# Weighted diagonals of a top-4 expert layer: made by GpSimd between its row gathers instead of by ScalarE

## The chip, the cores and the metric

The kernel runs on one core of a Trainium2 chip. The metric is the device time of one execution in microseconds (us); the kernel before took 1272.82 us, the median of three runs (1269.32 to 1274.13).

The engines are named as the profile names them: PE is TensorE, DVE is VectorE, ACT is ScalarE, POOL is GpSimd and SP is SyncE, which only starts transfers here. Each engine works through one queue in order. An instruction that waits holds up everything behind it on its own engine and nothing on the others, except those that need its result.

## The reference

The input is 2 sequences of 2048 rows of 128 numbers (float32). Three steps follow one another, each with a residual connection:

```
x = x + 0.5 * ffn(layernorm(x))      # first expert layer
x = x + ssm(layernorm(x))            # state space layer, 2 x 128 channels, 16 states
x = x + 0.5 * ffn(layernorm(x))      # second expert layer, same weights

# ffn, per row: 32 experts, 4 chosen
scores = softmax(row @ router_w.T + router_bias)
top4, idx = top_k(scores, 4);  top4 = top4 / top4.sum()
out = sum_k top4[k] * down[idx[k]](silu(gate[idx[k]] row) * up[idx[k]] row)
out = out + shared_expert(row)

# ssm: a scan along the sequence, per channel d and state s
h[d,s] = h[d,s] * exp(dt[d] * A[d,s]) + dt[d] * u[d] * B[s]
y[d]   = sum_s h[d,s] * C[s] + D[d] * u[d]
```

The scan carries its state from row to row, so the two sequences are each worked through in order. The expert layers have no such chain, but the experts of a group of rows can run only when all of its rows are sorted, and the results of a group can be collected only when all of its experts are done.

## The kernel before

The 4096 rows are 8 blocks of 512 (blocks 0 to 3 are the first sequence, 4 to 7 the second). A block is 4 tiles of 128 rows.

**An expert layer** (`mixture`, from line 689) handles the blocks in groups: (0,1), (2,3), (4,5,6,7) in the first layer and (0,1,2,3), (4,5), (6,7) in the second. For each group:

- PE makes the router's scores and DVE picks the best four and works out, for every row and choice, a slot in a list sorted by expert (lines 735 to 927). The weights `wk` of the four choices come out of this too.
- POOL writes every row to its four slots in memory: one indirect transfer per tile and choice, 128 rows each (`scatter`, L948; 16 per block, 256 in all).
- The experts run over the sorted list, four slots of 128 rows at a time: SP loads the rows (L1038) and the weights of the slots' experts (`fetch`, L1057, two experts into one buffer `wt`, of which there are 8), PE turns and multiplies (L1075, L1085, L1113), ACT and DVE apply silu and the product (L1097, L1103), SP stores the result (L1126).
- POOL fetches for every tile its four result rows, one indirect transfer per choice (`gather`, L1140; 256 in all), into `yg`.
- The four results of a row are weighted and added on PE: `weighed` (L1165) multiplies each gathered 128x128 block by a diagonal matrix that has the weights of that choice on its diagonal, and lets PSUM add the four products. The diagonal is the identity with each partition scaled by its weight. Four of them make a buffer `dg`, of which there are 2. `diagonal` (L1157) makes them on ACT, four activations per tile, 256 in all.
- DVE adds the sum to the block (L1176) and, in the first layer, takes the statistics for the next layernorm.

**The state space layer** (`state_space`, from line 1215) goes block by block. ACT and POOL make the steps `dt` and `dtu` (on POOL the three operations L1357 to L1359, twice per block). Then 16 states follow. For each, SP brings a row of B to all partitions (L1379), POOL multiplies it with `dtu` into a buffer `hst` (`drive`, L1389; 128 in all; 4 buffers), ACT makes the decays (L1401), DVE runs two scans (L1427) and one product (L1440), and PE adds the result to the output (L1206), which frees the buffer.

**The order.** No engine's order comes from a scheduler at build time. Every step is an operation of a planner (`op`), and the list `ORDER` (lines 48 to 242) gives the sequence in which all of them are issued. `RINGS` (line 39) gives the number of buffers of each kind. The steps that matter here are spread through the whole list: gathers and scatters stand between drives, and the expert layers overlap the state space layer at both of its ends.

**Pads.** A planner operation with a lag (scatter and gather) counts up a row; any other POOL operation sets it back to 0. From the third transfer in a row on, a small memset of a scratch tile (`pad`, L414) is put ahead of the transfer:

```
            if o.eng == "pool":
                row = row + 1 if o.lag else 0
                o.pause = row > 2
```

Of the kernel before, what the change touches and what calls it, by code (L numbers as in the profile page):

```python
# [13 lines left out]
ALU = mybir.AluOpType  # L14
# [6 lines left out]
TOPK = 4  # L21
# [4 lines left out]
TB = 4  # L26
# [15 lines left out]
    shb=1, sg=3, hs=4, xs=4, xT=3, h=3, wt=8, yq=3, yg=4, dg=2,  # L42
# [6 lines left out]
0 36 1 104 10 27 31 16 6 8 13 5 20 7 22 9 4 12 49 14 2 30 11 25 120-121 3 80 17 37 26 97 32 19 92 28 23 79 48 15 24  # L49
18 21 107 29 100 50 38 89 40 39 33 83 122-123 129-132 124 81 34 58 41 91 43 96 42 35 98 885-886 884 133 887 45-46  # L50
59-60 85 87 47 88 44 51 84 52 114 78 56 54 82 86 53 55 90 110 95 57 112 93 125-128 134-136 138 137 888 186-189 139
190-195 198 196 199 197 200 140 201 889 142 141 143-144 202-203 145-146 890-892 204-205 208 206 895 207 210 900 209
211-213 216 214 217-218 147 150 215 896 901 219 151-153 220-221 897 902 893-894 503 61 101 94 996 998 898-899 905
997 1000-1001 999 1002 1004 1003 502 1006 1005 1008-1010 1007 1011 906 903 148 904 907-908 149 99 909-910 504-506
911 1012-1013 912 1014 1016 1015 1017 915 1018 1020 1019 1021-1022 1024 1023 1026-1027 1025 1028-1030 916 914 913
917 1031 154 168 184 164 167 177 163 176 165 174 170 159 181 172 169 155 157 162 156 158 175 178 173 179 185 180 171
160 183 166 182 161 223 237 222 224 236 251 250 238 918-919 1032 1034 1033 1035-1036 1038 1037 1039-1040 1042 1041
1044-1045 921 1043 1046 511 1047 920 1048 922-924 1049 225 512 925-926 928 927 513 226 507 239 230 508 240 231-232
253-254 241-242 244 227 245 243 246 252 258 255 228 256 229 233 259 234 257 260 929-931 247 264 267 265 278 71
292-293 266 66 279 248 261-262 268 281-282 295-296 269-270 283-285 271 294 249 306 514-515 272-273 297-298 274 299  # L60
280 235 286-288 263 72 75 320 568 509 275 450 570 276 510 516 569 571 289 300-302 290 517 303-304 518-519 572 574
573 309-310 576 575 578 577 580-581 579 520-521 582-583 307 311-313 321 70 68 335 74 69 291 106 308 277 64 305 77
334 62 67 336 63 348 322 102 76 349 65 73 363 362 323 584 522 324 585 524 523 525-526 325-327 314-315 527-528 316
328-330 337-338 342-343 351 317-318 352 344 339-340 365-366 341 331-332 116 376 350 379-380 345 356 346 319 390 377
364 113 347 333 111 378 404 418 353-354 357 367-368 529 532 358 393 369 355 359 394 360 370-372 381-383 586 588
373-374 587 590 589 592 384 591 593 385-386 530 594 596 595 531 597 387-388 407 598 600 408 432 103 419 391 395-396
405 117 420 392 361 397 421 599 601 422 398-400 533 435-436 409-410 401 423-424 402 433 406 105 389 434 375 411-413
426-427 414 425 428 415-416 932 995 982 946 958 976 988 947 942 933 989 939 935 959 953 937 936 963 950 993 954 957
943 974 956 949 944 941 990 960 969 977 965 951 948 962 536 945 952 955 564 543 555 546 552 558 566 550 565 557 562
540 559 538 561 539 560 553-554 541 563 545 544 537 549 547 551 548 556 567 542 429-430 440 437 109 605 403 619 417  # L70
620 431 108 602 457 438 441-442 439 443-445 460 961 463 455 470 447 461 469 448 456 446 449 462 453-454 468 467 968
973 940 603-604 618 606 633 632 1050 1052 1051 1053-1058 1060 1059 1062 1061 1063-1067 607 621 608 622 609-611
626-627 612-613 628 614 646 660 647 661 634-635 623-625 636 615 629 649 616 630 650 663-664 640 637 641-642 674 648
631 662 688 702 617 675 651 638-639 652-656 665-666 668-670 667 451 677 119 691 678 464 692 452 458 643-644 657 459
471 465-466 658 671 705 472-473 706 672 1516-1517 679 689-690 676 703 716 645 693 115 659 704 673 730 696 680 694
681-682 697 1518 534 698 695 683 719 1519 478 720 684 710-711 1520 712 685 1521 492 686 1522-1524 699 707-708 700
744 1529-1530 758 731-732 717 1531 718 709 1525 1532 1526 474 483 476 938 491 495 484 934 481 475 482 477 994
488-489 971 497 490 981 966 498 496 713 733-734 714 1536 1533-1535 1537 479 1527-1528 747 485 480 748 724-725 486
1538 487 726 1539 1542-1544 1540 715 118 687 772 745-746 701 786 1550 1560 759-760 735 738 721 739 736 722 535 1545
740 737 723 1541 1546-1547 987 1551 761-762 727-728 493 741 775 494 499 776 500 742 501 729 1570 800 773-774 980  # L80
1561 986 975 1571 992 814 1580 801 1581 1590 1552-1553 749-750 766-767 839 751-753 1554-1555 768 1556-1557 754
763-764 1562 755 1563 789 1564 765 769 1548 756 1558 1720 790 1565-1567 1574 1572 1721 770 1568 1573 1575-1577 780
1549 777 1559 1569 803 1722 1582-1583 781 984 972 1591 802 815 1600 757 1610 771 787 743 1620 964 1601 970 979 1630
788 778 1584-1586 779 1587 782 1578 1592 1594 791 1579 1593 1595-1597 804 1602-1603 1605-1606 1723 1604 1589 1599
1607 1588 792 1612 783-784 1608 1598 1613 1724 1611 967 983 793 817 1614-1617 1621 985 1631 991 978 1622 818 1623
794 805 808 795 809 806 1625-1626 796 810 807 1632 1609 1619 1624 1627 797 811 816 1725 1634 798 1633 1635-1637 812
1642 1628 1618 1643 1097 1640 1069 1641 1650 1660 785 1070 799 1670 1068 1082 822-823 1645-1646 1651 819 1629 820
1726 1638-1639 1644 824 821 1647 1652 825 1655 1071 1654 1649 1085 826 1653 1648 1656 1072 1662-1663 1661 1665-1666
1729 1657 1086 1672 1671 1673 1727 1076 1664 1730 1667 1659 1073 1077 1658 1728 1074 1674 1733 1675-1676 1078 1075
1677 1682 1680 813 1681 1685 827 1683 1734 1079-1080 1736 1690 1096 1700 1692 1740 1678 1741-1742 1110 1735 1111  # L90
1124 1138 1081 1083 1754 1684 1686-1687 1669 1679 1689 1737-1738 1668 831 836 838 835 828-830 1691 851 837 1694 1099
1695 1743 1739 1746 1693 1100 1744 832 1696-1697 833 1704 1702 1747-1748 1699 1113-1114 1688 1703 834 1701 1705 1749
840-841 844 1764 1084 1098 1774 1087 1706 1090 1707 1104 1750 1088 1091 846 1745 843 1751 845 1755 842 849-850 852
1765 1709 853 1710 1105 1715 1092 1089 1106 1101-1102 1711-1712 1103 1756 1708 1757 1716-1717 1758 1093 1713
1759-1761 1718 1714 1719 1698 1094 1752 1766 1731 1767 1762 1732 847-848 1769-1770 1768 1753 1115 854 1763 1127 860
1116 1784 856 866 1775 871 855 1117 1771 1776 1924 1777 867 1925-1926 1128 1778-1781 1786 1772 1107 1787 1927 1108
1928 1794 1804 1773 1783 1141 1152 1788 1785 880 1795 1805 865 1789-1791 1796 1142 1782 1797 1929-1932 1798-1801
1806 1937 1808 1807 1809-1811 1938 1940 1792 1816 1944 1793 1945 1802 1817 1814 1125-1126 1112 1824 1815 859 863
857-858 1825 879 864 1129 1132 1139 1939 1109 1834 1166 1844 1854 1818-1821 1941 1130 1133 1118-1120 1131 1134
1826-1827 1829-1830 1803 1155 1813 1169 861 1823 1828 1835 1822 1812 1942-1943 1836 1156 1839 1831 862 1946 1170  # L100
1837 868 872 1845 1855 877 1840 1846 1121 1950 881 874 1122 1847 869 1832 1951 1864 1095 1180 1153 1140 1154 1874
1884 1194 870 873 878 1833 1838 1849-1850 1841 1933 1856 1952 1857 1842 1934 1135 1848 1143-1144 1859 1851 1866 1858
1843 1860 1145 1861 1953 1867 1862 1136 1954 1865 1157 1868 1935 1869-1871 1947 1875-1876 1158 1852 1936 1877 875
1853 1159 1879 876 882-883 1880 1886 1955 1146-1147 1160 1863 1878 1161 1123 1894 1167-1168 1904 1181 1208 1885 1137
1222 1182 1895 1889 1148 1162 1881 1887 1890 1873 1149 1183 1888 1408 1896 1872 1150 1184 1891 1897 1163 1948 2128
1164 1882 1898 1197 1174 1883 1899-1901 1906-1907 1198 1188-1189 1175 1905 1949 1893 1908 1171 1903 1172 2129
# [216 lines left out]
def macaron_kernel(  # L323
# [23 lines left out]
    nc = tc.nc  # L347
# [335 lines left out]
    def mixture(li, gi):  # L683
# [449 lines left out]
        for i, b in enumerate(blocks):  # L1133
            for t in range(TB):
# [20 lines left out]
                def diagonal(i=i, t=t, dg=dg):  # L1155
                    for k in range(TOPK):
                        nc.scalar.mul(  # L1157
                            dg.t[:, k, :], ident.t, route["wk"][:, i * TB + t, k : k + 1]
                        )
# [429 lines left out]
```

## Time and profile before

| | us |
|---|---|
| median of three runs | 1272.82 |
| the profiled execution, its own time | 1270.85 |
| its span (first to last instruction) | 1269.1 |
| PE busy | 999.6 |
| POOL busy | 996.7 |
| DVE busy | 853.0 |
| ACT busy | 817.2 |

The span is 1.75 us shorter than the execution's own time. Three of the POOL groups, out of the list of groups: 128 drives take 303.4 us, 382 pads 125.6 us and 256 gathers 247.1 us. On ACT the 256 diagonals take 80.7 us.

How such lines are read: "busy" is the time in which an engine's instructions ran, without its waits and its register work. A group is all instructions of one line and shape, with its summed time, the mean of one in nanoseconds, and the idle time of the engine just before its instructions with the work that ended that idle time. The chain of waits follows the end of the program back, at each step to what released it. The timeline lists one engine's instructions with the idle time ahead of each in square brackets; "issue" there means that the engine waited for nothing that the profile shows.

### The profile page before, as it was taken

How to read it: one execution, taken by the hardware profiler on the slowest of the kernel's cores; microseconds unless marked ns; L12 is line 12 of the kernel's file. 1: busy time of each engine (PE TensorE's matmuls, PEld its weight loads, DVE VectorE, ACT ScalarE, POOL GpSimd, SP SyncE). 2: the span in 40 equal slices, each digit the busy share in tenths (PEclk: the TensorE clock that was granted, in tenths of full speed). 3: DMA queues.
4: the chain of work that ended last, by engine and by line, in shares of the span. 5: the costliest groups of instructions: out<-in, count | busy, mean ns of one | idle time of the engine just before them, and what ended most of it. 6: DMA issues, size and time to landing. Idle time of an engine off the chain costs nothing.

```text
span 1269.1 us, 20680 instructions
## 1 busy us (share of the span) xinstructions
PE 999.6 (79%) x6276; PEld 811.2 (64%) x6290; DVE 853.0 (67%) x1567; ACT 817.2 (64%) x1578; POOL 996.7 (79%) x1088
## 2 busy tenths in 40 slices
PE   5968797877788787877858767588788886978986
PEld 3637676766566676765535545365678875868864
DVE  6764432259889999996499999999998534312221
ACT  3514442798798887975857866668788554535542
POOL 0768788899898655668899999878688358888886
PEclk9988998989898898998979897789899989989997
DMA  9899996886636674851213323132689987799932
GB/s 328 274 307 329 328 295 193 263 247 202 199 107 192 179 227 137 276 156 47 72 33 99 107 73 104 61 100 80 189 253 303 287 246 230 239 311 287 301 106 70
DMA packets 255985, 248.61 MB, mean 196 GB/s; under 512 B 24961, under 2 KB 223234, under 8 KB 255874
## 3 DMA queue, kind: packets, MB, share of 16 engines
q1 hardware_dynamic: 239490, 213.70, 54.6%
q0 software_dynamic: 16384, 33.59, 8.7%
q8 instruction: 51, 0.84, 0.3%
q14 instruction: 60, 0.49, 0.1%
HBM read 177.72 MB, written 69.47 MB: 195 GB/s over the span
## 4 chain that ended last, share of the span: by engine, by line
DVE 30%; PE 20%; POOL 14%; DMA 13%; ACT 9%; issue 9%; SPq 4%; POOLq 0%; DVEq 0%; ACTq 0%
DVE hst L1427 15%; POOL yg L1140 7%; PE gu L1085 7%; DVE hst L1440 4%; POOL pad L414 3%; PE oq L1113 3%; DMA yg<-ys,idx 3%; POOL xs L948 3%; PE sum L1165 3%; DMA wt<-w_dram 3%; ACT L420 2%; ACT da L1401 2%; DMA xs<-xs 2%; PE pt_x L1075 2%; DVE h L1103 2%
## 5 line engine op out<-in xcount | busy, mean ns | idle before, releaser
L1389 POOL TENSOR_TENSOR hst<-dtu,bs 128x1024 f32<-128x1024 f32 x128 | 303.4, 2377 | 70.2 <-PE y L1206 22.9
L1140 POOL DMA_INDIRECT yg<-ys,idx x256 | 247.1, 965 | 78.1 <-issue 40.1
L1085 PE MATMUL gu<-xT,wt 128*128 128x128 f32 x1792 | 249.7, 293 | 24.3 <-DMA wt<-w_dram 10.3
L1085 PEld LDWEIGHTS gu<-xT,wt 128*128 128x128 f32 x1792 | 234.0, 207 | 45.8 <-DVE h L1103 12.4
L948 POOL DMA_INDIRECT xs<-xn,idx x192 | 192.6, 1003 | 81.4 <-DMA hst<-in_up_w 34.1
L1427 DVE TENSOR_TENSOR_SCAN hst<-da,st,hst 128x512 f32<-128x512 f32 x192 | 237.5, 1269 | 5.3 <-ACT da L1401 3.0
L1401 ACT ACTIVATE da<-dt,a 128x512 f32<-128x512 f32 x256 | 174.6, 690 | 58.3 <-DVE hst L1427 55.2
L1103 DVE TENSOR_TENSOR h<-sgq,gu 128x256 f32<-128x256 f32 x224 | 88.6, 417 | 174.3 <-ACT sgq L1097 172.1
L420 ACT ACT_TABLE_LOAD x134 | 171.9, 1283 | 3.2 <-PEq L1577 0.8
L1206 PEld LDWEIGHTS y<-ident,hst 128*128 128x128 f32 x1024 | 127.7, 151 | 70.1 <-issue 38.0
L1440 DVE TENSOR_TENSOR hst<-hst,c 128x1024 f32<-128x1024 f32 x128 | 156.0, 1219 | 12.7 <-PE c L1413 2.7
L1206 PE MATMUL y<-ident,hst 128*128 128x128 f32 x1024 | 142.4, 289 | 25.0 <-DVE hst L1440 23.1
L1097 ACT ACTIVATE sgq<-gu 128x256 f32<-128x256 f32 x224 | 81.0, 384 | 117.5 <-PE gu L1085 113.9
L1113 PE MATMUL oq<-wt,h 128*128 128x128 f32 x896 | 125.1, 286 | 20.4 <-DVE h L1103 16.7
L1113 PEld LDWEIGHTS oq<-wt,h 128*128 128x128 f32 x896 | 113.4, 198 | 32.5 <-DVE h L1103 21.6
L414 POOL MEMSET pad<- 128x256 bf16 x382 | 125.6, 329 | 0.3
L1165 PE MATMUL sum<-yg,dg 128*128 128x128 f32 x512 | 85.7, 320 | 44.5 <-DMA yg<-ys,idx 34.2
L1165 PEld LDWEIGHTS sum<-yg,dg 128*128 128x128 f32 x512 | 78.3, 228 | 54.9 <-DMA yg<-ys,idx 19.8
L1075 PE MATMUL pt_x<-ident,xs 128*128 128x128 f32 x448 | 73.1, 294 | 43.2 <-DMA xs<-xs 28.1
L1078 ACT COPY xT<-pt_x 128x512 f32<-128x512 f32 x112 | 65.0, 584 | 50.4 <-PE pt_x L1075 50.1
L1157 ACT ACTIVATE dg<-ident,wk 128x128 f32<-128x128 f32 x256 | 80.7, 391 | 22.6 <-PE sum L1165 20.1
L1075 PEld LDWEIGHTS pt_x<-ident,xs 128*128 128x128 f32 x448 | 56.5, 152 | 56.6 <-DVE h L1103 15.8
(148 smaller groups left out, 1504.4 us busy)
## 6 DMA issues: line engine op xcount, KB each, us to landing
wt<-w_dram SPq DMA_DIRECT2D x448, 192.0 KB
bs<-bd SPq DMA_DIRECT2D x128, 256.0 KB
xs<-xs SPq DMA_DIRECT2D x112, 256.0 KB
ys<-yq SPq DMA_DIRECT2D x112, 256.0 KB
xs<-zero SPq DMA_DIRECT2D x56, 256.0 KB
w_dram<-hst SPq DMA_DIRECT2D x12, 512.0 KB
yg<-ys,idx POOLq DMA_INDIRECT x256
xs<-xn,idx POOLq DMA_INDIRECT x192
```

What stands on the lines that cost most here:

```text
L414: pool(nc.gpsimd.memset(pad, 0.0))
L420: nc.scalar.preload_act_table_set(name)
L948: nc.gpsimd.indirect_dma_start(out=xs_b.t, out_offset=bass.IndirectOffsetOnAxis(ap=route["idx"][:, i * TB + t, k : k + 1], axis=0), in_=xn ...
L1085: nc.tensor.matmul(gu.t[:, j, s, :], wt.t[:, s, j * H : (j + 1) * H], xT.t[:, s0 + s, :], start=True, stop=True,)
L1113: nc.tensor.matmul(o.t[:, s, :], h.t[:, s, :], wts[s // 2].t[:, s % 2, 2 * H :], start=True, stop=True,)
L1140: nc.gpsimd.indirect_dma_start(out=yg.t[:, k, :], out_offset=None, in_=ys_b.t, in_offset=bass.IndirectOffsetOnAxis(ap=route["idx"][:, i * ...
L1165: nc.tensor.matmul(sm_.t, dg.t[:, k, :], yg.t[:, k, :], start=(k == 0), stop=(k == TOPK - 1),)
L1206: nc.tensor.matmul(y[:, t, k * P : (k + 1) * P], src[:, k, t * P : (t + 1) * P], ident.t, is_transpose=True, start=start and k == 0 and t ...
L1389: nc.gpsimd.tensor_tensor(h.t[:, :, 1:], dtu.t, bs.t.unsqueeze(1).to_broadcast([P, ND, T]), ALU.mult)
L1401: nc.scalar.activation(da.t, dt.t[:, k, :], AF.Exp, scale=a_t.t[:, k, s : s + 1])
L1427: nc.vector.tensor_tensor_scan(h.t[:, k, 1:], da.t, h.t[:, k, 1:], 0.0 if ini else st_sb[:, k, s : s + 1], ALU.mult, ALU.add,)
L1440: nc.vector.tensor_tensor(h.t[:, :, :T], h.t[:, :, 1:], cb.t.unsqueeze(1).to_broadcast([P, ND, T]), ALU.mult,)
```

## The change

`diagonal` is issued on POOL instead of ACT, as four planner operations per tile instead of one, so that each of the four can stand between two transfers. Since a diagonal has no lag, it sets the row of transfers back, and pads fall away where it stands. `dg` gets 4 buffers instead of 2, `wt` 7 instead of 8, and the whole list `ORDER` is another one (the indices in it are new, because there are 192 more operations).

```diff
-    shb=1, sg=3, hs=4, xs=4, xT=3, h=3, wt=8, yq=3, yg=4, dg=2,
+    shb=1, sg=3, hs=4, xs=4, xT=3, h=3, wt=7, yq=3, yg=4, dg=4,
...
-0 36 1 104 10 27 31 16 6 8 13 5 20 7 22 9 4 12 49 14 2 30 11 25 120-121 3 80 17 37 26 97 32 19 92 28 23 79 48 15 24
+0 13 1 10 104 12 4 7 27 8 11 5 25 6 2 37 86 9 29 19 17 82 22 100 21 15 23 101 28 16 24 18 36 14 20 26 105 3 88 48 97
...
-                def diagonal(i=i, t=t, dg=dg):
-                    for k in range(TOPK):
-                        nc.scalar.mul(
-                            dg.t[:, k, :], ident.t, route["wk"][:, i * TB + t, k : k + 1]
+                for k in range(TOPK):
+
+                    def diagonal(i=i, t=t, k=k, dg=dg):
+                        pool(
+                            nc.gpsimd.tensor_scalar(
+                                dg.t[:, k, :],
+                                ident.t,
+                                route["wk"][:, i * TB + t, k : k + 1],
+                                None,
+                                ALU.mult,
+                            )
                         )
 
-                op("act", 1.1, diagonal, r=[wk_b, route_b], w=[dg])
+                    op("pool", 0.5, diagonal, r=[wk_b, route_b], p=[dg])
```

What the built program holds on POOL: 256 diagonals more and 115 pads instead of 382; drives, scatters and gathers are the same in number. On ACT the 256 diagonals are gone and there are 138 loads of activation tables instead of 134.

Some counts that the list alone does not show, from the built queue of POOL. "Behind" is the number of transfers that stand directly behind another transfer.

| stretch of POOL's queue | before: transfers / behind / pads / diagonals | after |
|---|---|---|
| first scatter to first drive | 146 / 1 / 143 / 0 | 148 / 27 / 88 / 32 |
| first drive to drive 28 | 46 / 12 / 11 / 0 | 44 / 7 / 0 / 33 |
| drive 28 to the first gather of group (4,5,6,7) | 0 / 0 / 0 / 0 | 0 / 0 / 0 / 10 |
| that gather to drive 64 (block 4) | 51 / 3 / 45 / 0 | 47 / 7 / 3 / 37 |
| drive 64 to drive 112 | 77 / 25 / 6 / 0 | 81 / 14 / 5 / 19 |
| drive 112 to the first gather of the second layer | 32 / 6 / 19 / 0 | 32 / 7 / 11 / 9 |
| that gather to the last gather | 160 / 1 / 158 / 0 | 160 / 44 / 8 / 111 |

On DVE, PE and ACT the order hardly moves against the scans: the DVE work issued ahead of any of the landmarks (every eighth state) differs by 3.5 us at most, by the mean durations of before, and PE's by 2.6 us. After the last drive of POOL there stand 15 more scatters of group (4,5) than before.

## Prediction

> **What bounds the kernel now.** I read the totals first, then the busy time by stage, then POOL's timeline, because the totals alone choose no engine: PE and POOL are both busy for 79% of the span. By stage (columns: stretch, its length, then the busy time of PE, weight loads, DVE, ACT and POOL, the granted clock, the DMA share and GB/s):
>
> ```profile
> 152.00:273.00 121.00, 104.99 (x691) 88.23 (x692) 36.02 (x96) 65.66 (x141) 107.86 (x160) 0.93 0.83 253
> 273.00:420.00 147.00, 112.71 (x715) 93.80 (x717) 134.21 (x161) 128.49 (x242) 132.82 (x97) 0.91 0.64 187
> 420.00:570.00 150.00, 124.46 (x888) 108.19 (x888) 143.47 (x159) 129.03 (x222) 92.88 (x44) 0.94 0.65 193
> 570.00:657.00 87.00, 61.86 (x319) 42.40 (x319) 55.20 (x182) 55.63 (x121) 77.30 (x106) 0.90 0.19 53
> 657.00:800.00 143.00, 105.26 (x515) 69.86 (x514) 137.97 (x146) 104.62 (x175) 131.49 (x88) 0.89 0.30 92
> 1028.00:1269.00 241.00, 187.95 (x1298) 168.80 (x1296) 62.06 (x201) 108.14 (x273) 205.04 (x318) 0.89 0.72 222
> ```
>
> From 273 to 800 DVE carries the scans and is 91 to 96% busy, except in the hole from 570 to 657, where it waits for gathers. In that hole and in the end from 1028 on POOL is at 85 to 89%. The rest of POOL's time there is no slack, as its timeline shows (start, duration, in brackets the idle time ahead):
>
> ```profile
> 1128.40 0.95 POOL L1140 DMA_INDIRECT yg<-ys,idx  x1 [0.16 <-issue]
> 1129.35 0.33 POOL L414 MEMSET pad<- 128x256 bf16 x1
> 1129.84 0.95 POOL L1140 DMA_INDIRECT yg<-ys,idx  x1 [0.16 <-issue]
> ```
>
> A transfer and its pad come round every 1.44 us, of which 0.16 is the start of a transfer after something else than a transfer. So POOL is full from 1028.0 to the end of its last gather at 1261. Two transfers in a row look like this:
>
> ```profile
> 296.23 1.00 POOL L948 DMA_INDIRECT xs<-dtu,idx  x1 [0.17 <-issue]
> 297.54 0.96 POOL L948 DMA_INDIRECT xs<-dtu,idx  x1 [0.30 <-issue]
> ```
>
> The second costs 0.30 + 0.96 = 1.26 in place of 1.11, so 0.15 more than one behind a pad, but 0.18 less than a transfer with its pad.
>
> **The price that decides: one diagonal on POOL (d).** No row shows this operation. The nearest rows (busy, mean in ns):
>
> ```profile
> L414 POOL MEMSET pad<- 128x256 bf16 x382 | 125.6, 329 | 0.3
> L1389 POOL TENSOR_TENSOR hst<-dtu,bs 128x1024 f32<-128x1024 f32 x128 | 303.4, 2377 | 70.2 <-PE y L1206 22.9 <-ACT st L1452 10.3 <-DVE h L1103 8.8
> L1359 POOL TENSOR_TENSOR dtu<-dt,u 128x512 f32<-128x512 f32 x16 | 21.2, 1326 | 1.3
> masks.py:199 POOL TENSOR_SCALAR_AFFINE_SELECT ident<-ident 128x128 f32<-128x128 f32 x1 | 0.3, 285 | 0.0
> ```
>
> Lower end: the select reads one 128x128 tile and writes one, 0.285 us. Upper end: a product of two tiles costs 1.326 us at 512 columns and 2.377 at 1024, that is 2.05 ns per column and 0.275 us fixed, so 0.54 at 128 columns. The diagonal reads one tile and one number per partition; it is the select with a second, tiny operand. I take the nearest row plus 0.045 for that operand: d = 0.33, and keep 0.285 to 0.54 for the range.
>
> The page "GPSIMD Engine Reference" of the Trainium skill, section 4.1 Engine selection, sends elementwise products to VectorE, but grants that GpSimd with one input is "roughly line-rate". By it d would lie near the select's end of my range, and the sum below at about -17 us.
>
> **The sum, stretch by stretch.** With the counts of POOL's queue above, a stretch costs 1.11 per transfer, 0.15 for each behind another, 0.33 per pad and d per diagonal; what both kernels have alike cancels.
>
> 1. End, from 1028: before 160 x 1.11 + 0.15 + 158 x 0.33 = 229.9 (the timeline shows 233.0). After 177.6 + 44 x 0.15 + 8 x 0.33 + 111 d = 186.8 + 111 d, at 0.33 223.5: **-6.4** (0.285: -11.4; 0.54: +16.9; even at 0.39).
> 2. First scatter to first drive: before 162.1 + 0.15 + 47.2 = 209.4, after 197.4 + 32 d = 207.9: **-1.5** (-2.9 to +5.2). From 152 on the chain of waits runs through it. The chain also holds 2.07 us of ACT's diagonals between 256 and 277, which leave; the first drive still waits for POOL, so I count only POOL's part.
> 3. First drive to drive 28: before 56.5, after 49.9 + 33 d = 60.8: +4.3 (+2.8 to +11.2). Cover: at 423 POOL waits 3.61 us for a free buffer, so it runs ahead of DVE by then; but around 355, where block 1 starts, it has no such lead. The chain loses 2.29 us of ACT's diagonals at 351.64. Taken: 4.3 - 2.3 = **+2.0**. The 10 diagonals of the next stretch lie in its 57 us of POOL's idle time (150 - 92.88) and cost nothing; without that cover, 3.3.
> 4. The hole: the chain leaves POOL at 612.94, after 30 gathers. Up to there before 42.7, after 35.3 + 19 d = 41.6: -1.1. ACT's diagonals at 623.23 (1.27 us) leave the chain: -1.3. Together **-2.4** (-3.2 to +1.6). POOL itself reaches drive 64 5.5 earlier (71.9 against 54.2 + 37 d = 66.4), so next in the way is DVE's own router work up to 656.85.
> 5. Drive 64 to 112: POOL +2.5 + 19 d = +8.7, of which 5.5 are paid by the lead of step 4 and the rest lies in POOL's idle time between 800 and 905 (84.08 of 105 busy). Taken: **0** (-2 to +6).
> 6. `wt` with 7 buffers instead of 8: SP waits 52.6 us in 27 waits for the PE work that frees them. A fetch may go out one buffer turn later, some 2 us (two buffers per quad, 24 quads in about 100 us up to 1028). PE waited only 11 times for weights. Taken: **+1** (0 to +10).
> 7. The 15 scatters now behind the last drive take 15 x 1.44 = 22 us of the 31.5 us that POOL waits idle before 1028: 0; without that cover they would push the end by as much.
> 8. What ACT is freed of (80.7 us) beyond the pieces named: 0, as ACT's waits are mostly for DVE and PE (55.2 us for scans, 113.9 for gate and up products).
>
> Sum: -6.4 - 1.5 + 2.0 - 2.4 + 0 + 1 = -7.3. The profiled execution took 1270.85, so 1263.6; it lies 2.0 below the median of the three, so against the median 1272.82 - 7.3 = **1265.5**, which I call 1265.
>
> A lock speaks against the change. The same operation on POOL (L1358) took 2.16 us at 638.35 and 1.27 at 645.94; the long one ran beside DVE's `ea` at 639.17, which took 1.89 against 0.66 at 631.92. So the two hold each other up. The page "SBUF — State Buffer", section "SBUF: two separate sides", calls the shared port pair "an exclusive lock", taken by a DVE operation with two SBUF inputs only against a GpSimd operation that reads SBUF; a diagonal reads, a memset does not. By it, if one diagonal in ten met such an operation and cost its full length, 8 us would come on top (an estimate from this page and d); I leave this out of the sum, since in the end from 1028 DVE's work mostly has one input from PSUM.
>
> **Rivals.**
> - *The diagonal is dearer and POOL slows down (slower).* POOL is the bound at the end, in the hole and before the first drive, so its extra time is paid nearly in full. At d = 0.42: +3.6, +1.4, 7.3 - 2.3 = +5.0, 0.6 - 1.3 = -0.7, step 5 +5 (its lead is down to 2.2), +1: +15, **1288**. The sum is zero near d = 0.36. For it: a second operand has to be fetched first, and the upper row is 0.54. Against: the select with one tile costs 0.285.
> - *The gain does not reach the end (no change).* In the end stage the gathers also wait for stored results, and DMA (0.72, up to 0.96 between 1120 and 1160) and PE (188 of 241 us) are near full with one weight buffer fewer. Then step 1 gives 0 and -7.3 + 6.4 = -0.9: **1272**; with step 6 at its upper end instead, -7.3 + 9 = +1.7: 1274.5. For it: the chain of waits in the end changes between POOL, PE and `wt`. Against: POOL itself idles nowhere there for more than 1.5 us.
> - *The diagonal is as cheap as the select (more gain).* -11.4, -2.9, 2.8 - 2.3 = +0.5, -1.9 - 1.3 = -3.2, 0 and 0: -17, **1256**.
> - That pads would stay is excluded by the count of the built queue (115 instead of 382).
>
> **Chances.** Forecast 0.29, cheaper diagonal 0.13, no change 0.24, dearer diagonal 0.34. A measurement of this kernel tells about 0.5% (6.4 us) from no change: faster 0.29 + 0.13 = 0.42, within 0.5% 0.24, slower 0.34. Range: the cheaper rival with its ACT share somewhat larger reaches down to 1249, and the dearer one up to d = 0.44 (0.02 more; the sum rises by 22.4 us from 0.33 to 0.42, so by 5) to 1293; beyond lie the upper bound of d and a starved weight stream, about 2 in 10.
>
> **What would show it.** The group `dg` on POOL: a mean of 330 ns bears out the price; above 360 the sum turns. The end from the first gather of the second layer to the last: 227 us by my sum (233.0 - 6.4) against 233.0. Transfer and diagonal should come round every 1.44 us, and the hole's 30 gathers should end 1 us earlier. SP's waits for PE at L1057 should stay near 52.6 us; if they grow and PE waits more for `wt`, step 6 was wrong. If DVE's busy time from 570 to 800 grows with the same operations, the lock was. The prediction is wrong altogether if the end stage starts later than 1028 by more than a few us, since my steps put nothing on what leads up to it.

## The result and the profile after

| | us |
|---|---|
| after, median of four runs | 1329.79 (1324.61 to 1333.58) |
| before, median of four runs beside them | 1271.07 (1266.83 to 1274.13) |
| ratio | 1.046, 95% interval 1.041 to 1.051 |
| the profiled execution of after, its own time | 1333.58 |
| its span | 1331.9 |

The kernel became slower by 4.6%, outside the range of the prediction, whose upper end was 1293. The forecast was a gain of 0.6%.

First the groups on POOL, from the list of groups of the kernel after (busy us, mean ns of one, idle time ahead):

```profile
L1148 POOL DMA_INDIRECT yg<-ys,idx x256 | 255.0, 996 | 72.4 <-issue 46.9 <-DMA wt<-w_dram 22.4 <-PE gu L1093 0.5
L1167 POOL TENSOR_SCALAR dg<-ident,wk 128x128 f32<-128x128 f32 x256 | 161.8, 634 | 10.1 <-PE sum L1180 2.4
L422 POOL MEMSET pad<- 128x256 bf16 x115 | 38.8, 337 | 0.1
```

A diagonal takes 0.634 us on average, nearly twice the 0.33 of the prediction. The pads have shrunk from 125.6 to 38.8 us, as the count of the queue said, but 161.8 us of diagonals have come.

The timeline of POOL in the end stage of the same run shows what this makes of the pace:

```profile
1189.93 1.01 POOL L1148 DMA_INDIRECT yg<-ys,idx  x1 [0.17 <-issue]
1190.97 0.62 POOL L1167 TENSOR_SCALAR dg<-ident,wk 128x128 f32<-128x128 f32 x1
1191.76 1.01 POOL L1148 DMA_INDIRECT yg<-ys,idx  x1 [0.17 <-issue]
```

A transfer and a diagonal come round every 1.83 us (1191.76 - 1189.93) where a transfer and a pad took 1.44. Of the difference, 0.29 is the diagonal against the pad and 0.10 is new: behind a diagonal the transfer itself takes 1.01 us in place of 0.95 to 0.96, and 0.04 more passes before the diagonal starts.

By stage (columns as in the prediction; the hole, then the end stage, both of after):

```profile
576.00:669.00 93.00, 67.14 (x298) 47.11 (x298) 46.28 (x148) 42.99 (x73) 80.31 (x94) 0.79 0.16 42
1052.70:1320.80 268.10, 189.77 (x1275) 170.29 (x1274) 62.52 (x194) 73.82 (x152) 231.57 (x279) 0.86 0.65 198
```

POOL is at 86% in both, as before, so it still is the bound; the stages are longer by what it has to do. Where the 62.8 us of span came from, by marks read from the timelines of both kernels:

| stretch | before | after | more |
|---|---|---|---|
| start to first drive | 273.3 | 272.1 | -1.2 |
| first drive to the hole | 296.4 | 303.8 | +7.4 |
| hole, up to drive 64 | 82.2 | 92.8 | +10.6 |
| drive 64 to the first gather of the second layer | 376.1 | 384.0 | +7.9 |
| from there to the end of the last gather | 233.0 | 268.1 | +35.1 |
| behind it | 8.1 | 11.1 | +3.0 |

SP's waits for the work that frees weight buffers have doubled, and TensorE now waits for diagonals (the first line is from SP's waits over the whole run, the second from the waits of the end stage; total, times, longest):

```profile
SPq L1065 <- PE oq L1121: 113.7, 35, 10.7
```

```profile
PEld sum L1180 <- POOL dg L1167: 25.0, 7, 9.9
```

### The profile page after: what moved, and what is told of

Read it like the earlier page. It is cut to its first block, busy times and chain, and to the rows that moved or that the text cites. A ratio compares the mean times of both kernels' runs of the same rounds, so it can differ in the third digit from the quotient of the medians.

```text
span 1331.9 us, 20430 instructions
## 1 busy us (share of the span) xinstructions
PE 1016.0 (76%) x6281; PEld 822.3 (62%) x6290; DVE 852.3 (64%) x1567; ACT 752.9 (57%) x1326; POOL 1078.7 (81%) x1077
## 5 line engine op out<-in xcount | busy, mean ns | idle before, releaser
L1148 POOL DMA_INDIRECT yg<-ys,idx x256 | 255.0, 996 | 72.4 <-issue 46.9
L1093 PE MATMUL gu<-xT,wt 128*128 128x128 f32 x1792 | 252.1, 295 | 34.1 <-DMA wt<-w_dram 15.1
L1167 POOL TENSOR_SCALAR dg<-ident,wk 128x128 f32<-128x128 f32 x256 | 161.8, 634 | 10.1 <-PE sum L1180 2.4
L1180 PE MATMUL sum<-yg,dg 128*128 128x128 f32 x512 | 94.7, 342 | 87.8 <-DMA yg<-ys,idx 54.6
L1180 PEld LDWEIGHTS sum<-yg,dg 128*128 128x128 f32 x512 | 84.8, 247 | 101.7 <-POOL dg L1167 42.1
L1121 PE MATMUL oq<-wt,h 128*128 128x128 f32 x896 | 128.1, 291 | 21.9 <-DVE h L1111 11.5
L1121 PEld LDWEIGHTS oq<-wt,h 128*128 128x128 f32 x896 | 117.7, 205 | 34.0 <-DVE h L1111 17.8
L1191 DVE TENSOR_TENSOR x<-x,sum 128x128 f32<-128x128 f32 x64 | 18.0, 283 | 142.6 <-PE sum L1180 142.4
L1130 ACT COPY yq<-oq 128x512 f32<-128x512 f32 x112 | 64.8, 586 | 64.8 <-PE oq L1121 62.6
```

The costliest lines, as they stand in the source:

```text
L1093: nc.tensor.matmul(gu.t[:, j, s, :], wt.t[:, s, j * H : (j + 1) * H], xT.t[:, s0 + s, :], start=True, stop=True,)
L1121: nc.tensor.matmul(o.t[:, s, :], h.t[:, s, :], wts[s // 2].t[:, s % 2, 2 * H :], start=True, stop=True,)
L1148: nc.gpsimd.indirect_dma_start(out=yg.t[:, k, :], out_offset=None, in_=ys_b.t, in_offset=bass.IndirectOffsetOnAxis(ap=route["idx"][:, i * ...
L1167: nc.gpsimd.tensor_scalar(dg.t[:, k, :], ident.t, route["wk"][:, i * TB + t, k : k + 1], None, ALU.mult,)
L1180: nc.tensor.matmul(sm_.t, dg.t[:, k, :], yg.t[:, k, :], start=(k == 0), stop=(k == TOPK - 1),)
```

## The experiments

Times of the later runs need one remark. They came from several chips. On number 6 and in the first measurement, whose chip isn't on record, the kernel before takes 1266 to 1273 us, on three others (numbers 3, 1 and 7) 1403 to 1415 us. I call the former the first sort of chip and the latter the second sort. Every ratio below is against the kernel before on the same chip in the same batch.

Three theories stood at the start. **Price:** the diagonal costs 0.63 us where POOL is the bound. **Order:** the new sequence and its buffers cost time whatever the diagonal costs. **Lock:** the diagonal is cheap and was held up by DVE. A fourth, **pace**, was formed after e12: the other engines stand still when POOL's transfers follow each other too closely.

### e1: the prices, measured by themselves

```diff
+    for _ in range(3):
+        for n in (1, 2, 4):
+            pool(
+                nc.gpsimd.tensor_scalar(
+                    probe.t[:, :n, :], ident.t.unsqueeze(1).to_broadcast([P, n, P]), iota_p.t, None, ALU.mult
+                )
+            )
+        pool(nc.gpsimd.tensor_scalar(probe.t[:, 0, :], ident.t, 0.25, None, ALU.mult))
+        pool(nc.gpsimd.tensor_tensor(probe.t[:, 0, :], ident.t, iota_p.t.to_broadcast([P, P]), ALU.mult))
+        pool(nc.gpsimd.tensor_copy(probe.t[:, 0, :], ident.t))
...
```

> The kernel before with short POOL operations put ahead of its first scatter, where POOL waits for some 34 us anyway; their results are not used. Price theory: a product with a number per partition costs about 0.62 us at 128 columns here too, where hardly anything else reads the shared port; from 128, 256 and 512 columns follow its fixed part and its part per column. Lock theory (VectorE holds it up in the changed kernel): about 0.3 us here. A select at 128 columns from a broadcast weight should cost 0.29 us as the identity's did, at 512 columns 0.6 us.

The kernel before with a few POOL operations at its start (also selects and memsets). Its groups by form:

```profile
L597 POOL TENSOR_SCALAR probe<-ident,iota_p 128x512 f32<-128x512 f32 x3 | 4.7, 1562 | 0.2
L597 POOL TENSOR_SCALAR probe<-ident,iota_p 128x256 f32<-128x256 f32 x3 | 2.8, 925 | 0.2
L606 POOL TENSOR_SCALAR_AFFINE_SELECT probe<-thr 128x512 f32<-128x512 f32 x3 | 1.9, 637 | 0.2
L597 POOL TENSOR_SCALAR probe<-ident,iota_p 128x128 f32<-128x128 f32 x3 | 1.8, 612 | 0.0
L601 POOL TENSOR_SCALAR probe<-ident 128x128 f32<-128x128 f32 x3 | 1.6, 530 | 0.3
L602 POOL TENSOR_TENSOR probe<-ident,iota_p 128x128 f32<-128x128 f32 x3 | 1.4, 464 | 0.3
L606 POOL TENSOR_SCALAR_AFFINE_SELECT probe<-thr 128x128 f32<-128x128 f32 x3 | 0.9, 294 | 0.2
L603 POOL COPY probe<-ident 128x128 f32<-128x128 f32 x3 | 0.9, 291 | 0.2
```

The product with a number per partition costs 612 ns at 128 columns, and (1562 - 612) / 384 = 2.47 ns per further column. It is dearer than the product of two operands with as many columns (464 on average). That average mixes two prices: two of the three products took 0.40 us, and the third took 0.59 while DVE worked on two tensors of its own:

```profile
6.56 0.40 POOL L602 TENSOR_TENSOR probe<-ident,iota_p 128x128 f32<-128x128 f32 x1
19.32 0.42 DVE L772 TENSOR_TENSOR lo<-lo,nmx 128x256 f32<-128x256 f32 x1
19.41 0.59 POOL L602 TENSOR_TENSOR probe<-ident,iota_p 128x128 f32<-128x128 f32 x1
```

The price of the diagonal's form holds away from the stages in question, so the lock is not what doubles it: 612 here, where DVE stood idle beside the first of the three (0.61 us), and 592 at least and 622 in the middle over all 256 in the kernel after. But single diagonals were held up there. Of some 215 diagonals that POOL's timeline of the kernel after lists one by one, 11 take 0.74 to 1.07 us, and ten of these run beside a DVE operation that reads two tensors, as here:

```profile
1206.17 0.91 POOL L1167 TENSOR_SCALAR dg<-ident,wk 128x128 f32<-128x128 f32 x1
1206.18 0.44 DVE L929 TENSOR_TENSOR eq<-eq,sc 128x256 f32<-128x256 f32 x1
```

Beyond 0.622 each, these 11 make 3.3 us in all. Select and copy, at 294 and 291, are the cheap ones. e1 itself took 1422.31 us in its single run, 1% above the kernel before beside it.

### e2 and e6: the new order with the diagonals on ScalarE

```diff
-                        pool(
-                            nc.gpsimd.tensor_scalar(
-                                dg.t[:, k, :],
-                                ident.t,
-                                route["wk"][:, i * TB + t, k : k + 1],
-                                None,
-                                ALU.mult,
-                            )
+                        nc.scalar.mul(
+                            dg.t[:, k, :], ident.t, route["wk"][:, i * TB + t, k : k + 1]
...
-                    op("pool", 0.5, diagonal, r=[wk_b, route_b], p=[dg])
+                    op("act", 0.5, diagonal, r=[wk_b, route_b], p=[dg])
```

> The changed kernel's order and buffers, with the diagonals back on ACT; the pads come back by their rule (382). Price theory: POOL's queue has its old price again, so 1265 to 1285 us. Order theory (the new order, or 7 weight buffers, costs a good part of the 59 us): 1300 us or more.

> The changed order and buffers with the diagonals on ACT once more. Price theory: within 1.5% of the kernel before on a chip with fast transfers. Order theory: 1.03 as on the slow one.

Chip 3, second sort: 1453.01 us, ratio 1.032 (1.026 to 1.038); repeated 1445.57, 1.023 (1.016 to 1.030). With POOL's diagonals gone and 387 pads back, the new order is slower than the old one there by some 2.5%.

### e3: the new order with a select for each diagonal

```diff
-                            nc.gpsimd.tensor_scalar(
-                                dg.t[:, k, :],
-                                ident.t,
-                                route["wk"][:, i * TB + t, k : k + 1],
-                                None,
-                                ALU.mult,
+                            nc.gpsimd.affine_select(
+                                out=dg.t[:, k, :],
+                                in_=route["wk"][:, i * TB + t, k : k + 1].to_broadcast([P, P]),
+                                pattern=[[-1, P]],
+                                compare_op=ALU.is_equal,
+                                fill=0.0,
+                                base=0,
+                                channel_multiplier=1,
```

> The changed kernel, each diagonal made by one select from the broadcast weight (128x128, one input read) instead of the product with the identity. Price theory: 0.29 us in place of 0.63 takes 256 x 0.34 = 87 us from POOL, of which the end (111), the hole (19 to 37) and the start (32) give back about 55: 1270 to 1285 us. Order theory: still above 1300. Lock theory: a select reads SBUF too and is held up as well, so about 1330.

The diagonal fell to 308 ns and a select with the transfer behind it takes 1.45 us (0.30 + 0.16 + 0.99), yet the kernel took 1435.63 us, 1.019 (1.014 to 1.023).

### e4: the diagonals on POOL in the old order

```diff
-                        nc.scalar.mul(
-                            dg.t[:, k, :], ident.t, route["wk"][:, i * TB + t, k : k + 1]
+                        pool(
+                            nc.gpsimd.tensor_scalar(
+                                dg.t[:, k, :],
+                                ident.t,
+                                route["wk"][:, i * TB + t, k : k + 1],
+                                None,
+                                ALU.mult,
+                            )
...
-                op("act", 1.1, diagonal, r=[wk_b, route_b], w=[dg])
+                op("pool", 1.1, diagonal, r=[wk_b, route_b], w=[dg])
```

> The kernel before, its own order and buffers, with only the engine of the diagonals changed: four products in a row on POOL where ACT had them. Price theory: 128 diagonals of 0.63 in the end stage are 81 us, less the pads that fall away behind them (up to two per tile, 64 x 0.33 = 21), and some 25 more before it: 1340 to 1370 us, slower than the changed kernel. Order theory: below 1310.

Chip 3: 1498.04 us, 1.063 (1.058 to 1.068). The old order puts the diagonals in rows beside the pads, of which 350 stay (twelve diagonals in a row took 7.00 us at 1254.44), and its end stage is 333 us long.

### e5 and e9: the changed kernel on the chips of the second sort

> The changed kernel itself, to have it on the same chip as the next three, since the chip of the last four had slower transfers (the kernel before took 1408 us there). Both theories: 1.046 of the kernel before where transfers are as fast as in the first profiles; where they are slow the price theory expects less (POOL bounds less of the time), the order theory about as much or more.

> The changed kernel once more, beside its neighbours. Price theory (a diagonal of 0.63 us sits in every stretch that GpSimd bounds): the closing expert stage takes about 268 us wherever it runs, as in the two runs so far (268.1 and 268.4), because GpSimd is busy through all of it. Where the kernel before needs 233 us for that stage the ratio is 1.04 to 1.05; where the kernel before needs about 300 us the ratio is about 0.97. Rival (the new order itself is the better one and only the first measurement was unlucky): ratio below 0.98 everywhere.

1370.89 us, ratio **0.971** (0.964 to 0.977), and 1369.66, **0.972** (0.967 to 0.978): faster than the kernel before. Its end stage took 268.4 us both times, as in the first measurement (268.1); in the kernel before (profile of e1) that stage took 300.5 in place of 233.0. So POOL's bound is the same on both sorts, and something else holds up the kernel before on the second.

It is not slower work of DVE, ACT or the DMA queues. In e1 the instructions of DVE and ACT sum to 853.5 and 819.4 us, against 853.0 and 817.2 in the kernel before on the first sort. The packets of the two DMA queues q0 and q1 took 56.7% of 1420.5 us on 16 engines, 805 us, against 63.3% of 1269.1, 803 us; so the slower transfers of which the expectation of e5 speaks are not seen. PE's sum does grow, from 999.6 to 1059.4 us, at a granted clock of 0.869 against 0.915; no run shows whether that is a cause or comes of the waits. Most of the rest is in the waits. DVE in e1, the kernel before with the probe, and in e9, the kernel after (total, times, longest):

```profile
DVE h L1129 <- issue: 163.7, 51, 10.9
DVE h L1129 <- ACT sgq L1123: 118.3, 53, 11.2
...
DVE x L1202 <- remote: 29.2, 6, 9.5
```

```profile
DVE h L1111 <- issue: 118.5, 56, 9.5
DVE h L1111 <- ACT sgq L1105: 81.2, 54, 8.9
```

DVE stands idle for 164 us before its SwiGLU products while nothing that the profile shows holds it up, and ScalarE has such waits too. In the kernel before on the first sort no such wait of DVE is in the list. Summed over DVE and ACT, idle time with no shown releaser ("issue" or "remote") is 3.3 us for the kernel before and 0.3 for the one after in the first comparison, but 390 in e1, 300 in e7 (the kernel before with one weight buffer fewer, below), 220 and 252 in e5 and e9, and 387 in e3.

### e7 and e8: the weight buffer and the sequence alone

e7 is the kernel before with `wt=7`; where an operation finds no free buffer, the next possible ones go ahead, otherwise the order stays. e8 is e2 with the old numbers of buffers, in the same manner.

```diff
-    shb=1, sg=3, hs=4, xs=4, xT=3, h=3, wt=8, yq=3, yg=4, dg=2,
+    shb=1, sg=3, hs=4, xs=4, xT=3, h=3, wt=7, yq=3, yg=4, dg=2,
```

> The kernel before with 7 weight buffers instead of 8 and nothing else; an operation whose buffer is not free yet is issued as soon as it is, the rest keeps its order. If the missing buffer is what the new order loses by: 1.02 to 1.03 of the kernel before. If it is the sequence itself: within 0.5%.

> The changed order with the diagonals on ACT and the old buffers (8 for weights, 2 for diagonals; what has no free buffer yet is issued later). If the missing weight buffer costs the 3% seen on the slow chip: near 1.00. If the sequence itself does: near 1.03.

e7: 1419.32 us, 1.005 (1.002 to 1.008); the weight buffer costs about 0.5%, some 7 us there. e8: 1450.76, 1.030 (1.022 to 1.038), as slow as with the new buffers. On the second sort it is the sequence with ScalarE's diagonals that costs, not the buffers.

### e10, e16, e11, e17: repeats for the split of order and price

> The changed kernel with each diagonal made by one select of about 0.30 us in place of the product of 0.63 us. Price theory: where the kernel before needs 233 us for the closing stage, the select kernel's transfers come every 1.46 us and its closing stage takes 225 to 240 us, so it is 25 to 50 us ahead of the changed kernel and at 0.99 to 1.02 of the kernel before. Where the kernel before needs about 300 us, it is bounded by something else and stays at about 296 us, ratio 1.02. Order theory (the new sequence costs time of its own): ratio 1.02 to 1.03 in both.

> The changed kernel with the select of 0.30 us in place of the product, once more. If the chip is one where the kernel before takes about 1270 us: price theory 0.99 to 1.02, the closing stage 220 to 240 us (its period is 1.46 us where the kernel before has 1.44), at least 0.02 below the 1.046 of the changed kernel and below the 1.033 of select and pad together. Order theory (the new sequence costs 2 to 3% of its own, as with the diagonals on ScalarE): 1.02 to 1.03 and a closing stage that is no shorter than before. If it is one where the kernel before takes about 1410 us: 1.02 as three times before.

> The changed kernel's sequence and its buffers, with the diagonals on ScalarE and a pad behind each pair of transfers as in the kernel before. Price theory: GpSimd has the work that it had, so 0.99 to 1.01 where the kernel before needs 233 us for the closing stage. Order theory: 1.02 to 1.03, as in the two measurements so far (1.032 and 1.023).

> The new sequence and buffers with the diagonals on ScalarE and the pads of the kernel before. Where the kernel before takes about 1270 us: price theory 0.99 to 1.01, order theory 1.02 to 1.03. Where it takes about 1410 us: 1.02 to 1.03 as before.

All fell on chips of the second sort: select 1.021 (1.014 to 1.028) and 1.022 (1.016 to 1.028); ScalarE 1.030 (1.024 to 1.035) and 1.025 (1.019 to 1.031). They confirm the earlier ratios and do not answer for the first sort.

### e12 and e18: pads of one column

```diff
-        pool(nc.gpsimd.memset(pad, 0.0))
+        pool(nc.gpsimd.memset(pad[:, :1], 0.0))
```

> The kernel before with pads of 1 column in place of 256: 0.10 us instead of 0.33 us each, 387 of them, so 88 us of GpSimd's busy time go and nothing else changes. Price theory: what stands between two transfers on GpSimd decides the stretches that it bounds; the closing stage loses 0.23 us for each of its 159 pads, 37 us, if GpSimd bounds all of it, and ends at 196 to 215 us where it took 233; ratio 0.96 to 0.98. Rival (the transfers themselves, not GpSimd's instructions, set the pace, and the pads stand in time that would be lost anyway): within 0.5%, or slower through crowded transfers.

> The kernel before with pads of 0.12 us in place of 0.33 us. Where the kernel before takes about 1270 us: price theory, with the slope of two and three pads (134 and 279 us for 387 and 774 pads of 0.31 us) carried to the other side, 0.90 to 0.96; pace theory (the transfers crowd the rest on every chip once they follow each other fast enough, and the pad is there for that): 1.00 to 1.10. Where it takes about 1410 us: 1.097 as before.

The 382 pads take 45.5 us in place of 125.6, so 80 us of POOL's work less, and 1.097 (1.092 to 1.103) and 1.104 (1.097 to 1.111): the price theory missed both times by sign, on the second sort of chip. POOL of e12 issues a transfer every 1.26 to 1.27 us:

```profile
1277.17 0.95 POOL L948 DMA_INDIRECT xs<-xn,idx  x1 [0.19 <-issue]
1278.12 0.13 POOL L414 MEMSET pad<- 128x1 bf16 x1
1278.43 0.96 POOL L948 DMA_INDIRECT xs<-xn,idx  x1 [0.19 <-issue]
```

Meanwhile the other engines stand still together. In the same run, from DVE's timeline, then from ACT's, then from PE's:

```profile
1287.43 0.42 DVE L1103 TENSOR_TENSOR h<-sgq,gu 128x256 f32<-128x256 f32 x1 [9.64 <-issue]
1313.85 0.21 DVE L908 CAST sl<-ejT 1x64 int32<-1x64 f32 x1 [26.00 <-remote]
```

```profile
1287.01 0.38 ACT L1097 ACTIVATE sgq<-gu 128x256 f32<-128x256 f32 x1 [10.49 <-issue]
1306.68 0.59 ACT L1122 COPY yq<-oq 128x512 f32<-128x512 f32 x1 [19.28 <-remote]
```

```profile
1287.90 0.48 PE L902 MATMUL ejT<-ident,ej 128*128 128x128 f32 x1 [7.51 <-DVE h L1103]
1307.32 1.11 PE L1075 MATMUL pt_x<-ident,xs 128*128 128x128 f32 x4 [18.93 <-ACT yq L1122]
```

TensorE has finished `ejT` at 1288.4, but DVE's `sl`, which has no other input, starts at 1313.85. POOL issues scatters nearly without a break meanwhile.

### e13 and e14: two and three pads in the kernel before

```diff
         pool(nc.gpsimd.memset(pad, 0.0))
+        pool(nc.gpsimd.memset(pad, 0.0))
```

> The kernel before with two pads of 256 columns wherever it has one, so that 0.65 us in place of 0.33 stand between two of GpSimd's transfers; the diagonals stay on ScalarE and the order stays. Price theory (GpSimd's work adds up in the stretches that it bounds): slower, 159 pads by 0.31 us, up to 49 us, in the closing stage and some in the others, ratio 1.02 to 1.05. Pace theory (on this chip the other engines stand still while transfers follow each other at less than about 1.8 us, which is why the slow diagonal was the best and the short pad the worst): faster, 0.96 to 0.98, and the idle time that ends without a releaser in DVE's, ScalarE's and TensorE's rows is at least halved.

> The same with three pads, 0.97 us between two transfers. Price theory: 1.05 to 1.10. Pace theory: the stalls are nearly gone, but GpSimd now needs 2.1 us per transfer; the closing stage's 113 gathers, 31 scatters and their pads take about 144 x 2.1 = 300 us, as long as the stage takes in the kernel before on this chip, so 0.97 to 1.02, and slower than two pads.

These ran on a chip of the first sort: 1402.97 us, **1.106** (1.100 to 1.113), and 1545.14, **1.219** (1.211 to 1.226). There the price theory has the sign right and its upper ends too low (1.05 and 1.10). The speed-up that the pace theory expects does not come; but that theory was formed on the second sort, and the stalls on which it rests are absent here, so these runs don't test it where they occur. POOL of e13 in the end stage:

```profile
1250.54 0.95 POOL L1141 DMA_INDIRECT yg<-ys,idx  x1 [0.16 <-issue]
1251.49 0.33 POOL L414 MEMSET pad<- 128x256 bf16 x1
1251.88 0.31 POOL L415 MEMSET pad<- 128x256 bf16 x1
1252.34 0.95 POOL L1141 DMA_INDIRECT yg<-ys,idx  x1 [0.15 <-issue]
```

The second pad ends 0.37 us after the first (0.06 gap, 0.31); the period rises from 1.44 to 1.80 or 1.83. The stage has 158 pads, so 57 to 62 us were to come, and it grew by 64.2 (297.2 against 233.0); with three pads by 123.1 (356.1). Over the whole run 382 pads of 0.37 us are 141 us, and the kernel grew by 137. No other engine gives any of it back, and DVE and ACT together have 1.7 and 1.1 us of idle time with no shown releaser.

### e15: the new order with select and pad, as slow together as the product

```diff
                                 channel_multiplier=1,
                             )
                         )
+                        pool(nc.gpsimd.memset(pad, 0.0))
```

> The changed kernel's order with the select of 0.30 us and one pad of 0.31 us behind it: together what the product took, 0.63 us. Pace theory: equal to the changed kernel, 0.965 to 0.98, though the select alone was at 1.02 three times over and this adds work to it. Price theory and order theory: slower than the select alone, 1.02 to 1.06.

On the same chip of the first sort: 1312.27 us, 1.033 (1.027 to 1.040); as the price theory has it, and again without stalls (0.6 us). From its timeline:

```profile
1154.09 0.95 POOL L1148 DMA_INDIRECT yg<-ys,idx  x1 [0.30 <-issue]
1155.05 0.30 POOL L1167 TENSOR_SCALAR_AFFINE_SELECT dg<-wk 128x128 f32<-128x128 f32 x1
1155.29 0.32 POOL L1177 MEMSET pad<- 128x256 bf16 x1
1155.77 0.99 POOL L1148 DMA_INDIRECT yg<-ys,idx  x1 [0.17 <-issue]
```

Select and pad overlap by 0.06: from the end of a gather (1155.04) to the start of the idle time ahead of the next (1155.60) pass 0.56 us. In the kernel after it is 0.65 (1190.94 to 1191.59). Over the 111 diagonals of the end stage those 0.09 us make 10 us, and the stage is 11.2 us shorter (256.9 against 268.1).

## Why the prediction was wrong

The failed step is "The price that decides: one diagonal on POOL (d)". It took d = 0.33, the select plus 0.045 "for that operand", with 0.54 as the upper end. The runs show 0.634 in place and 0.612 alone. Both thoughts behind it failed. The diagonal is not a select with a second, tiny operand: even with a plain number in place of the pointer the product takes 0.530 (e1). And a product of two operands is no upper end for one with a single tile: 0.464 on average, 0.40 undisturbed, against 0.612 (e1). The measured price lies 0.07 to 0.09 above the upper end, so the range failed with it. The Trainium skill's page "GPSIMD Engine Reference", section 4.1 Engine selection, calls GpSimd with one input "roughly line-rate"; for this operation the measurement decides: 2.47 ns per column against 0.89 for the select ((637 - 294) / 384).

The form of the sum was right in the main. Its five steps that hold d count 111 + 32 + 33 + 19 + 19 = 214 diagonals; 214 x (0.634 - 0.33) = 65, and 1265.5 + 65 = 1330.6 against 1329.8 measured. That it comes so close is partly luck: with the true price steps 2 and 3 charge too much and steps 1, 4 and 5 too little, as they show one by one:

- **Step 1, the end.** 186.8 + 111 x 0.634 = 257.2, and 111 x 0.10 for the transfers behind a diagonal, 268.3; seen 268.1. That it fits to 0.2 is luck, as the same form gave 229.9 where before shows 233.0. The mechanism was right and the price wrong: +35.1 in place of -6.4. The extra 0.10 was a second miss; the sum had the same 1.11 for every transfer.
- **Step 2, first scatter to first drive.** With the true price +8.2; seen -1.2 at the first drive, or +0.7 from the first scatter, which came 2.0 earlier. The sum left out POOL's own waits for other work in this stretch (those not marked "issue"): 14.3 us in before, 8.5 of them ahead of the second group's first scatter, against 5.0 in after. So idle time covered the diagonals.
- **Step 3, first drive to the hole.** With the true price 2.0 + 33 x 0.304 = +12; seen +12.5 at drive 28 (409.1 - 273.3 = 135.8 us before, 148.3 after), where POOL runs nearly without a wait, so the price was paid in full. Of this, 5.1 came back by the hole, where POOL has idle time: +7.4 in all.
- **Step 4, the hole.** POOL up to drive 64: 54.2 + 37 x 0.634 + 37 x 0.10 = 81.4 against 71.9, +9.5; seen +10.6 in place of -2.4. The lead on which step 5 was to live never came.
- **Step 5, drive 64 to 112**, taken at 0 (-2 to +6), and **step 7, the 15 scatters**, at 0: together +7.9, and it is step 5 that failed. The gather that opens the end stage needs the experts of group (0,1,2,3), and these need the group's last scatter. The last scatter and the first work of the experts on its rows, before and after:

```profile
880.14 0.97 POOL L948 DMA_INDIRECT xs<-xn,idx  x1 [0.16 <-issue]
887.36 0.63 PE L1075 MATMUL pt_x<-ident,xs 128*128 128x128 f32 x4 [1.11 <-DMA xs<-xs]
```

```profile
907.16 1.01 POOL L956 DMA_INDIRECT xs<-xn,idx  x1 [0.18 <-issue]
913.38 0.63 PE L1083 MATMUL pt_x<-ident,xs 128*128 128x128 f32 x4 [1.63 <-DMA xs<-xs]
```

  From drive 64 to that scatter it was 228.3 us and is 238.5: +10.2. The lead of 5.5 us that was to pay for this stretch did not exist, and its diagonals cost twice the price. From the scatter to the gather it was 147.9 and is 145.5, so the 15 scatters of group (4,5), which stand behind all this, pushed nothing. POOL still has idle time behind them:

```profile
1028.02 1.01 POOL L1140 DMA_INDIRECT yg<-ys,idx  x1 [31.50 <-DMA xs<-xs]
```

```profile
1052.69 1.04 POOL L1148 DMA_INDIRECT yg<-ys,idx  x1 [22.24 <-DMA wt<-w_dram]
```

  e15, the same order with cheaper diagonals, shows the same split: 237.4 and 144.9.
- **Step 6, the weight buffer**, taken at +1 (0 to +10). SP's waits did grow, from 52.6 to 113.7, against what the prediction said. But 54.5 of them lie behind 1030 (17.3 in before), where TensorE itself waits for diagonals, and e13 has 77.8 with 8 buffers and two pads, so a good part of the growth follows POOL. PE's own waits for `wt` grew from 10.3 to 15.1 us. e7 puts the buffer itself at 0.5% on the second sort of chip.
- **Step 8, ACT's relief** at 0: nothing seen speaks against it.

Of the rivals, "the diagonal is dearer" came true, with a price beyond its bounds. What the prediction said of a lock against the change was seen, but small: about one diagonal in twenty was held up, by some 0.3 us, in place of the one in ten at full length that it tried out, so 3.3 us in place of 8. That the DVE operation beside it is the cause is read from the overlaps, not tried. DVE's busy time did not grow (852.3 us against 853.0), and the price alone in e1 is nearly the price in place. The warning on what would make the prediction wrong altogether came true as well: the end stage started 24.7 us later than before.

What stays open: whether the sequence costs anything of its own on the first sort of chip, since the select without a pad and the diagonals on ScalarE never ran there. From e15, taking off 0.25 us (0.56 less 0.31 for the select alone) for 148 diagonals in the end and the hole, 37 us, the select would come to some 1275 us, near the kernel before. By ratio e15 lies 0.013 below the changed kernel, 16 us for 256 x 0.09 = 23 us of diagonals; at that share the 0.25 us would give back some 45, and the select would come to 1267. Both are estimates, and the order could cost a few us by them or none. None of the kernels run on the first sort beats the kernel before; on the second the changed kernel beats it and every other.

Open too is why the two sorts differ. On the second, two single edits point the same way, shorter pads (1.10 against 1) and shorter diagonals (the select's 1.02 against 0.97): there the closer POOL's transfers follow each other, the slower the kernel. The idle sums of DVE and ACT follow this at the two ends, 220 and 252 us for the changed kernel and 492 and 567 for the short pads, but not between: the kernel before with 300 (e7) to 390 (e1) and the new order with ScalarE's diagonals (304 to 348) differ by 2 to 3% in time, and the select with 377 to 390 is faster than the latter. More pads were not tried there, no row shows what the engines lack in that time, and it isn't shown that it is a property of the chips rather than of the time at which they were used.

## What to carry to other kernels

Before work is moved to an engine that bounds the time, measure that very operation on it, in its form and shape, by a probe of a few instructions: a "nearest row" of another form was off by a factor of two here, and the sign hung on it. Idle time of an engine ahead of a wait covers moved work as long as what it waits for doesn't depend on that work, as with the 15 scatters; a lead that is worked out with a wrong price covers nothing, as in step 5. A ratio of a few per cent from one chip may have the other sign on the next, so look for idle time without a releaser before trusting either.

## What the runs showed of the hardware

- On GpSimd a product with one number per partition takes 612 ns for 128 columns of f32 and 2.47 ns for each further column; with a plain number 530, a product of two operands some 400, a select 294, a copy 291 (e1).
- Beside a DVE operation that reads two tensors, the product of two operands took 0.59 us in place of 0.40 (e1), and single diagonals took up to 1.07 us in place of 0.62 (the kernel after).
- In the end stage a gather behind such a product takes 1.01 us, behind a pad's memset 0.95 to 0.99 (before, after, e15).
- The kernel before took 1266 to 1273 us in two batches and 1403 to 1415 on three other chips, with 3.3 us of idle time of DVE and ACT without a releaser in the one and 390 (with the probe) in the other, while the instructions of both took as long (1670 us in the one, 1673 in the other).
